# Last chunk of a two-layer AdaLN kernel: each tile's first expert leaves PSUM through ScalarE, the other seven stay on VectorE

## The chip, the cores and the metric

The kernel runs on one core of one Trainium2 chip. The metric is device time in microseconds, the median of five executions. One further execution was taken with the hardware profiler; its rows are what the working below is made from. Engines are named as in the profile: PE (TensorE matmul), PEld (its weight load), DVE (VectorE), ACT (ScalarE), POOL (GpSimd), SP (SyncE; SPq is its DMA queue).

## What is computed

Two layers, each of the form x + gate * attention(norm(x)), then x + gate * mixture(norm(x)), on x of 4 x 1024 x 256 floats. The change sits in the last mixture, that of layer 1:

```
def _L1_ffn_ref(hidden_states, router_w, expert_weights):
    x = hidden_states.reshape(-1, H)
    probs = softmax(x @ router_w.T)
    topk_vals, topk_idx = top_k(probs, 2)
    topk_w = topk_vals / (topk_vals.sum(-1) + 1e-06)
    expert_out = einsum('nh,eho->eno', x, expert_weights)     # 8 experts, 256 x 256 each
    combined = the two chosen experts' rows of expert_out
    out = ((combined + their probs) * topk_w).sum(over the two)
...
x = x + gb * _L1_ffn_ref(h, ...)
```

For a token the result is a sum over the two chosen experts of weight times row, plus one number per token (the two probabilities times their weights), times the gate.

## The kernel before, in words

Tokens are handled in 8 chunks, numbered 0 to 7, of 4 tiles; a tile is 128 tokens (one on each partition) of 256 features, one for each of the four batch rows b. `x_sb` holds all of x on the chip.

Layer 1's mixture goes two ways. Chunks 0 to 3 (group "ga") and 4 to 6 (group "gb") are **routed**: their normalised rows are written to DRAM (`ga_rows`, `gb_rows`), sorted by expert into blocks of 128, and each block is fetched by a gather, multiplied by one expert's weights (PE, L2276), copied out of PSUM by ACT (L2286) and stored to DRAM (`gb_y`, SP, L2289). When all blocks of a group are stored, `combine` takes every tile back: two gathers on POOL (L332) fetch each token's two rows into a buffer `yg`, ACT scales the first and adds the bias (L1504), and DVE adds the second (L1510), multiplies by the gate (L1513) and adds into `x_sb` (L1515). Then SP stores the chunk (L2464, 512 KB). There are five `yg` buffers; group gb has 12 tiles, so 24 gathers.

Chunk 7 is **dense** (function `dense`): for each of its four tiles, PE multiplies by all eight experts, two at a time, into a PSUM tile `p_e` of 2 x 256 (L2324, four groups j of four matmuls per tile; three such PSUM buffers). DVE takes the experts out one after the other into a tile `step`: expert 0 by a TENSOR_SCALAR that multiplies by the token's weight `d_w` and adds the bias `d_vb` (L2340), experts 1 to 7 by a SCALAR_TENSOR_TENSOR that multiplies by the weight and adds the running sum (L2349). Then `done` multiplies by the gate and adds into `x_sb` (L2369, L2370) and SP stores the tile (L2373, 128 KB). There are two `step` buffers, so tile b needs tile b - 2 to be done.

The order on every engine is fixed when the kernel is built. A planner (`Plan`) holds pieces of work, each with an engine, a cost in us, the pieces it comes after, the buffers it holds and a rank; it plays them through and emits the instructions in the order in which the pieces would begin. Each engine then works its own list in that order, and semaphores hold an instruction whose input is not ready. The costs in the planner only decide the order. Dense tiles and the combines of chunks 4 to 6 are interleaved on DVE in this way.

Of the kernel before, what the change touches and what calls it, by code (L numbers as in the profile page):

```python
# [11 lines left out]
AF = mybir.ActivationFunctionType  # L12
ALU = mybir.AluOpType
# [6 lines left out]
P = 128  # L20
B, S, D = 4, 1024, 256
# [117 lines left out]
def adaln_d2_kernel(  # L139
# [20 lines left out]
    nc = tc.nc  # L160
# [10 lines left out]
    def psum(pool, shape, name):  # L171
        tag = {id(ps_1): "p1", id(ps_2): "p2", id(ps_m): "pm"}[id(pool)]
        t = pool.tile([P, 512], F32, tag=tag, name=name)
        n = 1
        for s in shape[1:]:
            n *= s
        v = t[: shape[0], :n]
        if len(shape) == 3:
            v = v.rearrange("p (a b) -> p a b", b=shape[2])
        return v  # L180
# [61 lines left out]
    rank = const.tile([P, E], F32, name="rank")  # L242
# [636 lines left out]
    plan = Plan(p1=3, p2=2, pm=3, xn1=5, h1T=2, xn2=6, h2T=2, t1=1)  # L879
    PE, ACT, DVE, POOL = "PE", "ACT", "DVE", "POOL"  # L880
# [408 lines left out]
    ps = plan.slot("p1")  # L1289
# [27 lines left out]
    for half in range(2):  # L1317
        ps = plan.slot("p1")
# [11 lines left out]
        m = plan(PE, 0.3, turn, after=routes, holds=[ps], rank=rank_)  # L1330
# [6 lines left out]
    for piece in range(3):  # L1337
        ps = plan.slot("p2")
        m = loaded
        for k in range(KD):  # L1340
# [12 lines left out]
            m = plan(PE, 0.87, mm, after=[m, of_batch["routed"]], holds=[ps], rank=20.0)  # L1353
# [5 lines left out]
    ps = plan.slot("p1")  # L1359
    d = of_batch["turned"]  # L1360
    m = plan(PE, 0.2, lambda: g0.total_staged(ps_1), after=[d], holds=[ps], rank=-1.0)
    ps2 = plan.slot("p1")

    def bases():
# [8 lines left out]
        after=[m2],  # L1373
        holds=[ps2],
        rank=-0.9,
    )
    ps = plan.slot("p1")
    m = plan(PE, 0.4, lambda: g0.across(ps_1), after=[d], holds=[ps], rank=-1.0)
# [3 lines left out]
    for j in range(AHEAD):  # L1382
        ps = plan.slot("p1")
# [12 lines left out]
        m = plan(PE, 0.25, look, after=[r], holds=[ps], rank=first)  # L1396
        plan(DVE, 0.6, find, after=[m], holds=[ps], rank=first)
        kept_busy(0.7 if j < AHEAD - 1 else 2.0, [m], 30.0 + j)
    with tc.manual_schedule(engines=ORDERED):
# [36 lines left out]
        step=2,  # L1436
# [6 lines left out]
    made = {}  # L1443
# [7 lines left out]
    def tiny(shape, tag, n=2, dt=F32):  # L1451
        return home["tiny"].tile(shape, dt, tag=tag, name=tag, bufs=n)
# [310 lines left out]
    plan = Plan(rings=RINGS, **room1)  # L1763
# [184 lines left out]
    plan = Plan(rings=RINGS, **room1)  # L1948
# [199 lines left out]
    def shares(g, c, at, vb, x, rank):  # L2148

        key = ("m", c)  # L2150

        def do():
            x = made[key, "x"]
            down = tiny([P, B, E + 1], "rdown")
            nc.vector.tensor_scalar(down, x, -1.0, 1.0, ALU.mult, ALU.add)
            nc.vector.reciprocal(down, down)
            nc.vector.scalar_tensor_tensor(x, x, 1.0, down, ALU.add, ALU.mult)
            p = tiny([P, 2, B], "rp")
            nc.vector.tensor_reduce(p[:, 0, :], x[:, :, :E], AX.X, ALU.add)
            nc.vector.reciprocal(p[:, 0, :], p[:, 0, :])  # L2160
            nc.vector.tensor_tensor(
                p[:, 1, :].unsqueeze(2), x[:, :, E : E + 1], p[:, 0, :].unsqueeze(2), ALU.mult
            )
            total = tiny([P, B], "rtotal")
            nc.vector.scalar_tensor_tensor(
                total, p[:, 0, :], 1e-6, p[:, 1, :], ALU.add, ALU.add
            )
            nc.vector.reciprocal(total, total)
            w = g.w[:, :, at : at + B]
            nc.vector.tensor_tensor(  # L2170
                w, p, total.unsqueeze(1).to_broadcast([P, 2, B]), ALU.mult
            )
            nc.vector.tensor_tensor(p, p, w, ALU.mult)
            nc.vector.tensor_tensor(vb[:, at : at + B], p[:, 0, :], p[:, 1, :], ALU.add)

        return plan(DVE, 2.2, do, after=[x[0]], holds=[x[1]], rank=rank)
# [119 lines left out]
    def dense(c, slotT, ts, d, x, rank):  # L2296

        key = ("d", c)
        g = last_pairs
        vb = tiny([P, B], "d_vb", 1)  # L2300
        x = shares(g, c, 0, vb, x, rank)

        def spread_w():
            w = made[key, "w"] = tiny([P, B, E], "d_w", 1)
            v = tiny([P, B, E], "d_v", 1)
            for i, t in ((0, w), (1, v)):
                nc.vector.tensor_tensor(
                    t,
                    g.one[:, i, :, :],
                    g.w[:, i, :].unsqueeze(2).to_broadcast([P, B, E]),  # L2310
                    ALU.mult,
                )
            nc.vector.tensor_tensor(w, w, v, ALU.add)

        x = plan(DVE, 0.6, spread_w, after=[x, d], rank=rank)
        for b in range(B):
            last, st = [], plan.slot("step")
            for j in range(E // 2):
                ps = plan.slot("p1")

                def mm(b=b, j=j):
                    p1 = made[key, b, j] = psum(ps_1, [P, 2, D], "p1_e")
                    for k in range(KD):
                        nc.tensor.matmul(  # L2324
                            p1,
                            lhsT=made["n2", c, "hT"][:, k, b, :],
                            rhs=ew[:, 2 * j : 2 * j + 2, k, :],
                            start=(k == 0),
                            stop=(k == KD - 1),
                        )  # L2330

                def out_(b=b, j=j):
                    if j == 0:
                        made[key, "sum", b] = tiny([P, D], "step")
                    w, sum_ = made[key, "w"], made[key, "sum", b]
                    for i in range(2):
                        e = 2 * j + i
                        p = made[key, b, j][:, i, :]
                        if e == 0:
                            nc.vector.tensor_scalar(  # L2340
                                sum_,
                                p,
                                w[:, b, e : e + 1],
                                vb[:, b : b + 1],
                                ALU.mult,
                                ALU.add,
                            )
                        else:
                            nc.vector.scalar_tensor_tensor(  # L2349
                                sum_, p, w[:, b, e : e + 1], sum_, ALU.mult, ALU.add  # L2350
                            )

                m = plan(
                    PE, 1.74, mm, after=ts, holds=[ps, slotT], rank=rank + 0.1 * b + 0.02 * j
                )
                last = [
                    plan(
                        DVE,
                        0.95,
                        out_,  # L2360
                        after=[m, x, *last],
                        holds=[ps, st],
                        rank=rank + 0.1 * b + 0.02 * j - 0.5,
                    )
                ]

            def done(b=b):
                sum_, xs = made[key, "sum", b], x_sb[:, c, b, :]
                nc.vector.tensor_tensor(sum_, sum_, mods1[GB][:, b, :], ALU.mult)  # L2369
                nc.vector.tensor_tensor(xs, xs, sum_, ALU.add)  # L2370

            def store(b=b):
                nc.sync.dma_start(out[b, c * P : (c + 1) * P, :], x_sb[:, c, b, :])  # L2373

            f = plan(DVE, 0.9, done, after=last, holds=[st], rank=rank + 0.1 * b)
            plan(SP, 0.1, store, after=[f], rank=rank)
# [10 lines left out]
    for c in range(NC):  # L2387
# [26 lines left out]
        if c == NC - 1:  # L2414
            d, x = routed(last_pairs, c, 0, slotT, ts, 7.46)
            dense(c, slotT, ts, d, x, 8.23)
            continue
        g, first = groups[which], 4 * which
        at = (c - first) * B
        d, x = routed(g, c, at, slotT, ts, c + 1.05)  # L2420
# [108 lines left out]
```

## Time and profile before

| | us |
|---|---|
| median of 5 executions | 1129.64 (1128.33 to 1131.09) |
| the profiled execution: device time | 1129.15 |
| the profiled execution: span, first to last instruction | 1127.4 |
| PE busy in the span | 1088.8 (97%) |
| DVE busy | 588.2 (52%) |
| ACT busy | 424.5 (38%) |
| POOL busy | 422.2 (37%) |

All times of the profile count from the start of the span. A group's row gives line, engine, operation, output and inputs, the tile's shape, the count, and the mean duration. Consecutive instructions of an engine overlap by some 0.1 us, so that the distance from start to start is a little off the duration. PE's shares are those of the whole span; the stretch that the change touches is the last 45 us, where PE ends at about 1113.5 us.

### The profile page before, as it was taken

To read this page: it belongs to the slowest core of one execution; us is meant where nothing else is said; L and a number is where in the kernel's file an instruction comes from. 1 tells how busy PE (TensorE), PEld (TensorE's weight loads), DVE (VectorE), ACT (ScalarE), POOL (GpSimd) and SP (SyncE) were. 2 spreads that over 40 slices of the span, in tenths; PEclk is the share of its full clock that TensorE was granted. 3 is DMA by queue.
4 is the path that set the end of the run, shared out by engine and by line. 5 is a ranking of instruction groups with operands and counts; after the bars stand their busy time and mean duration, and the time that the engine had idled before them with its cause. 6 is when DMAs were issued, how large, how long until landed. Compare 5 with 4: busy or idle time off the path is not lost.

```text
span 1127.4 us, 18450 instructions
## 1 busy us (share of the span) xinstructions
PE 1088.8 (97%) x6231; PEld 867.7 (77%) x6231; DVE 588.2 (52%) x2305; ACT 424.5 (38%) x1148; POOL 422.2 (37%) x483
## 2 busy tenths in 40 slices
PE   8999999999999999999999999999999999999994
PEld 5896899999999999999989565675656667656761
DVE  7777332222222222222256488968577635698567
ACT  6976233332233322333244333423224425342431
POOL 1000455555555555555554010100114422654635
PEclk9999999999999999999999999999999999999998
DMA  9424449433331514242161221100003323432544
GB/s 320 162 54 95 151 143 315 149 117 113 100 130 38 189 39 150 78 145 86 38 238 54 72 57 57 60 25 19 1 31 97 117 71 82 133 117 75 167 108 147
DMA packets 77692, 122.38 MB, mean 109 GB/s; under 512 B 27340, under 2 KB 57301, under 8 KB 72990
## 3 DMA queue, kind: packets, MB, share of 16 engines
q0 software_dynamic: 31872, 69.68, 19.6%
q1 hardware_dynamic: 44622, 49.92, 13.8%
q10 hardware_dynamic: 1104, 1.58, 0.4%
q8 instruction: 52, 0.85, 0.3%
q14 instruction: 42, 0.34, 0.1%
HBM read 205.25 MB, written 30.22 MB: 209 GB/s over the span
## 4 chain that ended last, share of the span: by engine, by line
PE 83%; DVE 8%; DMA 4%; ACT 2%; issue 2%; SPq 1%; POOL 0%; DVEq 0%; ACTq 0%
PE p_h L1658 20%; PE p_y L1681 20%; PE p_u L1967 19%; PE p_f L2015 10%; PE p_e L2276 4%; PE pm_x L2259 1%; PE pm_x L1638 1%; DMA w<-in_W,g_wrow 1%; PE pm_l L2107 1%; PE pm_t L1620 1%; PE pm_counts L737 1%; PE pm_l L1233 1%; PE pm_o L1193 1%; DVE yg L1510 1%; DVE step L2349 1%
## 5 line engine op out<-in xcount | busy, mean ns | idle before, releaser
L1670 ACT ACTIVATE hid<-p_h,w 128x128 f32<-128x128 f32 x544 | 154.9, 368 | 326.4 <-issue 249.0
L1658 PEld LDWEIGHTS p_h<-xT,w 128*128 128x128 f32 x2176 | 253.1, 192 | 5.8 <-DVE xT L1643 1.9
L1658 PE MATMUL p_h<-xT,w 128*128 128x128 f32 x2176 | 254.4, 275 | 1.9 <-DVE xT L1643 1.3
L1681 PE MATMUL p_y<-w,hid 128*128 128x256 f32 x1088 | 248.9, 382 | 0.0
L1967 PE MATMUL p_u<-hT,a 128*128 128x512 f32 x512 | 230.8, 595 | 1.1 <-ACTq L1930 0.8
L1681 PEld LDWEIGHTS p_y<-w,hid 128*128 128x128 f32 x1088 | 201.6, 190 | 24.6
L1967 PEld LDWEIGHTS p_u<-hT,a 128*128 128x128 f32 x512 | 94.3, 190 | 97.7 <-issue 88.3
L332 POOL DMA_INDIRECT w<-in_W,g_wrow x134 | 135.0, 1008 | 74.7 <-ACT hid L1670 46.9
L784 POOL DMA_INDIRECT y<-y,g_dest x68 | 69.5, 1022 | 146.9 <-DVE g_reached L724 111.8
L1643 DVE COPY xT<-pm_x 128x256 f32<-128x256 f32 x68 | 28.8, 424 | 179.5 <-PE pm_x L1638 179.5
L1692 DVE TENSOR_TENSOR y<-p_y,w 128x256 f32<-128x256 f32 x68 | 28.8, 424 | 175.8 <-PE p_y L1681 175.8
L2015 PE MATMUL p_f<-a,hf 128*128 128x256 f32 x512 | 116.1, 380 | 0.0
L332 POOL DMA_INDIRECT xg<-h_rows,g_row x68 | 66.7, 980 | 122.9 <-DVE g_hits L750 102.5
L2015 PEld LDWEIGHTS p_f<-a,hf 128*128 128x128 f32 x512 | 96.2, 190 | 17.7 <-issue 5.7
L2063 POOL TENSOR_TENSOR x_sb<-x_sb,step 128x256 f32<-128x256 f32 x32 | 24.4, 764 | 173.5 <-DVE step L2056 120.5
L332 POOL DMA_INDIRECT xg<-ga_rows,ga_row x39 | 37.2, 954 | 91.4 <-DVE ga_row L759 35.0
L2276 PE MATMUL p_e<-ew,xT 128*128 x280 | 70.5, 384 | 0.3 <-ACT y L2286 0.3
L1979 ACT ACTIVATE hf<-p_u,decay 128x512 f32<-128x512 f32 x56 | 38.1, 684 | 78.2 <-PE p_u L1967 74.5
L2276 PEld LDWEIGHTS p_e<-ew,xT 128*128 128x128 f32 x280 | 49.3, 190 | 9.5 <-issue 3.5
L1578 DVE TENSOR_TENSOR h<-h,mod 128x256 f32<-128x256 f32 x128 | 51.4, 426 | 8.2 <-ACT h L1568 5.9
L1983 DVE SCALAR_TENSOR_TENSOR hf<-p_u,decay,hf 128x512 f32<-128x512 f32 x56 | 41.9, 748 | 22.7 <-PE p_u L1967 15.4
L2286 ACT COPY y<-p_e 128x256 f32<-128x256 f32 x70 | 25.9, 371 | 59.6 <-PE p_e L2276 27.9
(362 smaller groups left out, 1281.6 us busy)
## 6 DMA issues: line engine op xcount, KB each, us to landing
yg<-y SPq DMA_DIRECT2D x32, 256.0 KB, 2.5
ga_y<-y SPq DMA_DIRECT2D x39, 128.0 KB, 1.7
x_sb<-in_x SPq DMA_DIRECT2D x8, 512.0 KB, 7.5
h_rows<-xn SPq DMA_DIRECT2D x8, 512.0 KB, 3.5
gb_y<-y SPq DMA_DIRECT2D x31, 128.0 KB, 1.8
out_x<-x_sb SPq DMA_DIRECT2D x7, 512.0 KB, 3.6
a<-in_fw SPq DMA_DIRECT2D x6, 512.0 KB, 9.5
mod<-mod_rows SPq DMA_DIRECT2D x6, 512.0 KB
```

The costliest lines, as they stand in the source:

```text
L332: return nc.gpsimd.indirect_dma_start(out=dst, out_offset=None, in_=table, in_offset=bass.IndirectOffsetOnAxis(ap=index, axis=0), bounds_c ...
L784: nc.gpsimd.indirect_dma_start(out=table, out_offset=bass.IndirectOffsetOnAxis(ap=dest, axis=0), in_=y, in_offset=None, bounds_check=2 * s ...
L1578: nc.vector.tensor_tensor(h, h, mods1[(sc, sh)[i]][:, b, :], (ALU.mult, ALU.add)[i])
L1643: nc.vector.tensor_copy(xT, pt)
L1658: nc.tensor.matmul(p1[:, i, :], lhsT=w1[:, k * H + m * P : k * H + (m + 1) * P], rhs=xT[:, k, :], start=(k == 0), stop=(k == KD - 1),)
L1670: nc.scalar.activation(hid[:, m, :], p1[:, i, :], AF.Relu, bias=w1buf[j % 2][:, KD * H + m : KD * H + m + 1],)
L1681: nc.tensor.matmul(p2, lhsT=hid[:, m, :], rhs=w2[:, m * D : (m + 1) * D], start=(m == 0), stop=(m == KH - 1),)
L1967: nc.tensor.matmul(pu, lhsT=a[:, k, m * P : (m + 1) * P], rhs=made["n1", c, "hT"][:, k, :, :], start=(k == 0), stop=(k == KD - 1),)
L1979: nc.scalar.activation(made[key, m], made[key, m, 0], AF.Silu, scale=decays[c])
L1983: nc.vector.scalar_tensor_tensor(h, made[key, m, 1], decays[c], h, ALU.mult, ALU.mult)
L2015: nc.tensor.matmul(made[key, "p2", b], lhsT=made[key, m][:, b * P : (b + 1) * P], rhs=a1[:, m, :], start=(m == 0), stop=(m == KH - 1),)
L2276: nc.tensor.matmul(made[key, "p2"], lhsT=made[key, "xT"][:, k, :], rhs=ew_flat[:, bass.ds(made[key, "at"] + k * D, D)], start=(k == 0), st ...
```

## The change

In `dense`, expert 0 of each of the four tiles is no longer taken out of PSUM by DVE. A new piece `begin` on ACT does it: one ACTIVATE (Identity) with the token's weight as scale and the bias as bias, both one number per partition, from PSUM into `step`. It is planned at 0.45 us, after the first matmul group and the shares, and holds the same PSUM and `step` buffers. DVE's piece for j = 0 comes after it and holds one instruction (expert 1) in place of two; its planned cost goes from 0.95 to 0.48.

```diff
+                def begin(b=b):
+                    sum_ = made[key, "sum", b] = tiny([P, D], "step")
+                    nc.scalar.activation(
+                        sum_,
+                        made[key, b, 0][:, 0, :],
+                        AF.Identity,
+                        bias=vb[:, b : b + 1],
+                        scale=made[key, "w"][:, b, 0:1],
+                    )
+
                 def out_(b=b, j=j):
-                    if j == 0:
-                        made[key, "sum", b] = tiny([P, D], "step")
                     w, sum_ = made[key, "w"], made[key, "sum", b]
                     for i in range(2):
                         e = 2 * j + i
                         p = made[key, b, j][:, i, :]
-                        if e == 0:
-                            nc.vector.tensor_scalar(
-                                sum_, p, w[:, b, e : e + 1], vb[:, b : b + 1],
-                                ALU.mult, ALU.add,
-                            )
-                        else:
+                        if e:
                             nc.vector.scalar_tensor_tensor(
                                 sum_, p, w[:, b, e : e + 1], sum_, ALU.mult, ALU.add
                             )
...
+                if j == 0:
+                    last = [
+                        plan(ACT, 0.45, begin, after=[m, x], holds=[ps, st],
+                             rank=rank + 0.1 * b - 0.5)
+                    ]
                 last = [
                     plan(
                         DVE,
-                        0.95,
+                        0.95 if j else 0.48,
                         out_,
                         after=[m, x, *last],
                         holds=[ps, st],
```

In the order that the planner then emits, everything up to the dense chunk stands as before. On ACT the four new instructions (L2334 in the changed file) stand ahead of the last L2286 copy, behind the first combine's L1504, between those of the third and the fourth, and behind that of the seventh. On DVE the four L2340 are gone, and near the end two pieces move up: `done` of the third dense tile goes ahead of the tenth combine, and `done` of the fourth ahead of the eleventh, so that the list ends with two combines. POOL, PE and SP keep their order.

More of the change, by code (lines that the diff above doesn't have):

```diff
@@ L2338, in out_ @@
                         p = made[key, b, j][:, i, :]
-                        if e == 0:
[L2340 to L2346, printed above, removed]
-                            )
-                        else:
+                        if e:
                             nc.vector.scalar_tensor_tensor(
@@ L2355, in dense @@
                 )
+                if j == 0:
+                    last = [
+                        plan(
+                            ACT,
+                            0.45,
+                            begin,
+                            after=[m, x],
+                            holds=[ps, st],
+                            rank=rank + 0.1 * b - 0.5,
+                        )
+                    ]
                 last = [
```

## The prediction

> **What bounds the kernel now.** I read the page first (PE is busy 97% of the span, so only the end can belong to another engine), then the windows of the last 45 us, then the chain of waits and the timelines of DVE, POOL, ACT and SP there. The windows (stretch and length; busy us of PE, PEld, DVE, ACT, POOL; PE clock; DMA share; GB/s):
>
> ```profile
> 1085.00:1091.00 6.00, 6.00 (x17) 2.84 (x16) 3.13 (x7) 0.37 (x1) 1.96 (x3) 1.00 0.15 47
> 1091.00:1110.00 19.00, 18.56 (x44) 7.93 (x42) 17.89 (x42) 4.80 (x8) 14.67 (x15) 1.00 0.46 138
> 1110.00:1123.00 13.00, 1.95 (x4) 0.68 (x4) 11.97 (x28) 2.40 (x4) 6.80 (x7) 0.78 0.48 151
> 1123.00:1127.40 4.40, 0.00 (x0) 0.00 (x0) 0.00 (x0) 0.00 (x0) 0.00 (x0) 0.50 0.36 121
> ```
>
> Up to 1091 PE sets the pace; from 1091 to 1123 DVE is full; then only the last store runs. The DVE timeline (start, duration) shows where the four removed instructions sit and what surrounds them:
>
> ```profile
> 1084.89 0.54 DVE L2340 TENSOR_SCALAR step<-p_e,d_w,d_vb 128x256 f32<-128x256 f32 x1
> 1085.47 0.48 DVE L2349 SCALAR_TENSOR_TENSOR step<-p_e,d_w,step 128x256 f32<-128x256 f32 x1
> 1087.29 1.00 DVE L2349 SCALAR_TENSOR_TENSOR step<-p_e,d_w,step 128x256 f32<-128x256 f32 x2 [1.33 <-PE p_e L2324]
> ...
> 1092.56 0.53 DVE L2340 TENSOR_SCALAR step<-p_e,d_w,d_vb 128x256 f32<-128x256 f32 x1
> 1093.13 0.48 DVE L2349 SCALAR_TENSOR_TENSOR step<-p_e,d_w,step 128x256 f32<-128x256 f32 x1
> ...
> 1110.35 0.54 DVE L2340 TENSOR_SCALAR step<-p_e,d_w,d_vb 128x256 f32<-128x256 f32 x1
> ...
> 1121.35 0.48 DVE L1510 SCALAR_TENSOR_TENSOR yg<-yg,gb_w 128x256 f32<-128x256 f32 x1
> ...
> 1122.32 0.43 DVE L1515 TENSOR_TENSOR x_sb<-x_sb,yg 128x256 f32<-128x256 f32 x1
> ```
>
> In the first tile DVE then waits for PE, so time saved there is handed to that wait. From 1092.56 on DVE waits for nobody. But a second row of work runs beside it to almost the same end. POOL's gathers (in brackets: idle time before, and who ended it) and ACT's last step:
>
> ```profile
> 1088.43 0.95 POOL L332 DMA_INDIRECT yg<-gb_y,gb_slot  x1 [13.80 <-DMA gb_y<-y]
> ...
> 1116.56 1.00 POOL L332 DMA_INDIRECT yg<-gb_y,gb_slot  x1 [0.30 <-DVE yg L1510]
> 1117.86 1.01 POOL L332 DMA_INDIRECT yg<-gb_y,gb_slot  x1 [0.30 <-issue]
> ```
>
> ```profile
> 1119.58 0.60 ACT L1504 ACTIVATE yg<-yg,gb_vb,gb_w 128x256 f32<-128x256 f32 x1 [2.11 <-DMA yg<-gb_y,gb_slot]
> ```
>
> The answer for the tile yg adds how long a gather takes from issue to landing:
>
> ```profile
> DMA to landing us min/median/max: 2.7/2.8/3.3
> ```
>
> POOL never stops: 24 gathers, always 0.30 us apart whoever is named for it, 29.43 us from first start to last, 1.28 each. They start when the last block is stored and depend on no DVE work that this change makes later. The last gather starts at 1117.86 and lands between 1120.56 and 1121.16, by the median at 1120.66. DVE takes its rows at 1121.35. So DVE ends the kernel, with only 0.2 to 0.8 us between it and the gathers. That is the number that the forecast turns on.
>
> **The change, step by step.** *Removed on DVE.* Four L2340, 0.57 us from start to next start (1092.56 to 1093.13). All on the path they would be worth 2.3 us. Tile by tile:
> - Tile 1: ACT begins when DVE did, 1084.89 or some hundredths later (both need `d_w`). Its duration is in no row of before. Nearest are L1504, 0.60 us (same size, both operands from memory, SBUF source), and L1019, 0.77 us (PSUM source, both operands, twice the elements); from below the L2286 copy, 0.37 us (PSUM source, no operands). I take 0.57, the 0.60 row less a little, since only the source differs. Expert 1 then starts at about 1085.5, as before, and DVE waits for PE at 1087.29 anyway. Gain 0.
> - Tile 2: PE's groups release DVE at 1087.29, 1089.00 and 1090.72 in the timeline, 1.72 apart, so the next is ready at 1092.44. ACT runs 1092.44 to 1093.01 (free since its L1504 at 1091.14), DVE continues at about 1093.03 instead of 1093.13. Gain 0.1; between 0.3 (0.37 row) and -0.1 (0.77 row).
> - Tiles 3 and 4: PE is ahead (their first groups are ready four and eight groups of 1.72 later, near 1099.3 and 1106.2; DVE wants them at 1100.4 and 1110.35). ACT fits in: for tile 3 at 1099.3; for tile 4 after the `step` buffer of tile 2 is freed, its `done` ending at 1109.1 less the 0.67 gained by then, so 1108.5 to 1109.1, while DVE is busy with the seventh combine until 1109.7. Gain 0.57 each.
>
> DVE's sum is 0 + 0.1 + 0.57 + 0.57 = 1.24 us: it would be ready for the last combine at 1121.35 - 1.24 = 1120.1.
>
> *Added on ACT.* Four instructions on an engine busy 2.40 of the last 13 us. What queues behind them: the last L2286 copy behind the first, L1504 steps behind the others. The copy matters, since its store starts the gathers, and a late start would move the whole gather row one for one. It ran at 1085.61, when PE had finished its block. ACT starts the next instruction of this kind 0.50 us after the last (two L1568 in a row took 1.10), so it is free at 1085.4; even at the 0.77 row it is free at 1085.6. Cost 0, covered by that PE wait by 0.2 us. Tile 3's step delays the fourth L1504 from 1098.87 to about 1099.9, ending 1100.5; DVE wants it at 1100.7. Cost 0, covered by 0.2.
>
> *PE* waits 2.0 us for a PSUM buffer before its last group (1111.55); that buffer comes free 1.24 us sooner, the group ends near 1112.3, and DVE wants it at 1113.65. Nothing gained, nothing lost.
>
> *What is late next.* With the new order DVE's tail reads: ninth combine 1114.57, `done` of tile 3 at 1115.88, tenth combine 1116.68, `done` of tile 4 at 1117.99, eleventh combine 1118.79, free 1120.10 (1.31 per combine, 0.80 per `done`, the distances of before). The last combine then waits for the last gather; before, `done` of tile 4 stood there and hid that wait. The gather lands at 1120.66 by the median. SP's stores move too: tile 4's 128 KB go out at 1118.8 instead of 1121.5, so they now meet the last gather on the DMA engines; the store of the chunk before, 512 KB, goes from 1115.0 to 1113.9 and meets the gathers of the eleventh combine, which have over 0.6 us to spare by the median. The gather issued at 1116.56 flew right behind that 512 KB store and its ACT step began at 1119.58, 3.02 us later. I take 3.02 for the last one: 1117.86 + 3.02 = 1120.88, against 1121.35. **Gain 0.47 us**, between 0.79 (2.7) and 0.19 (3.3). What follows, three instructions and the last 512 KB store from 1122.77 to 1127.4, is unchanged.
>
> Span 1127.4 - 0.47 = 1126.9; with the 1.75 us around it, 1128.7 for that execution, which lay 0.49 under the median. On the median: 1129.64 - 0.47, about **1129.2**.
>
> [...] The 3.3 us maximum above is the trace's word on such meetings; without any meeting the sum would be 0.69, with a bad one 0.19.
>
> **Rivals.** (1) *The gather row also gets shorter, faster by more.* Gathers last 0.944 to 1.187 us; at the shortest throughout, 23 x 1.25 = 28.75 instead of 29.43, so the last starts 0.68 sooner, and the end comes up to 0.47 + 0.68, about 1.15 us sooner, near DVE's own 1.24: 1128.5. For it: less DVE work beside POOL. Against: the removed instructions read PSUM, and no row shows that they slowed a gather. (2) *The last gather lands late, slower than before.* Place: the last combine, behind tile 4's store and the gather. Price: its start less 1121.35. It decides from 3.49 us after issue. The worst in the answer is 3.3; with the excess over the median doubled (two stores met, tile 3's and tile 4's) it is 3.8, and the end 0.3 us later: 1129.9. Against: no row of that answer reaches 3.49. (3) *DVE's saving counts in full, 2.3 us*, 1127.3: excluded for tile 1 by its PE wait, and it would need the gathers another 1.2 us sooner than in rival 1.
>
> **How the numbers follow.** Forecast case (end set by the last gather, 0.2 to 0.8 us gained) 0.65; rival 1, 0.15; rival 2, 0.18; rival 3, 0.02. All but rival 3 are smaller than 0.2% (2.26 us), about what a measurement of this kernel can tell from no change; the five times of before spread over 2.8 us, so a median of five is good to about 1 us either way. The range takes rival 1 and 1 us below (1127.5) and rival 2 and 1 us above (1130.9). Beyond 0.2% only rival 3 or an unlucky pair of medians: faster 0.07, slower 0.04, within 0.89.
>
> **What would show it.** In the changed profile: no TENSOR_SCALAR on `step`; four ACT rows of about 0.57 us; DVE still waiting for PE in tile 1; PE's wait of 2.0 us shrunk to about 0.8; and, the main sign, an idle time of 0.5 to 1.1 us on DVE before the last L1510, ended by the gather's DMA, and POOL still at 1.28 per gather from 1088.4. If DVE shows no such idle time and the end is 1.2 us sooner, the gather bound is wrong; if the first gather starts after 1088.6, the ACT copy was delayed; if the last gather's rows come after 1121.35, rival 2 holds.

## The result, and the profile after

| | us |
|---|---|
| median before (46 executions) | 1129.99 |
| median after (25 executions) | 1129.55 |
| ratio after/before, 95% interval | 0.9995 [0.9989, 1.0002] |
| profiled execution after: span | 1127.9 |

The medians differ by 0.44 us where 0.47 was forecast. The interval, from 1.2 us faster to 0.2 us slower, does not tell that from no change, so it is luck that the two numbers lie so close. The finer evidence is in the profile, one execution of each kernel.

Its span is 0.5 us longer than that of before, and this must be read first: the token weights (DVE, L2313) start at 1085.39 instead of 1084.59. The order of work up to there is the same in both kernels, so those 0.80 us are the difference of two executions, not the change (the kernel before with one gather more, a run below with the same work up to there, has them at 1085.29). The comparison needs an event that both share: I count from T0, the start of the first gather of `yg`, 1088.43 before and 1089.22 after (3.84 and 3.83 us behind the token weights). The first and the last gather of the changed kernel, on POOL (start, duration, what; in brackets the idle time before):

```profile
1089.22 0.95 POOL L332 DMA_INDIRECT yg<-gb_y,gb_slot  x1 [13.79 <-DMA gb_y<-y]
...
1118.68 1.01 POOL L332 DMA_INDIRECT yg<-gb_y,gb_slot  x1 [0.30 <-issue]
```

The windows of the end of the changed kernel (stretch and length; busy us of PE, PEld, DVE, ACT, POOL; PE clock; DMA share; GB/s):

```profile
1091.00:1110.00 19.00, 19.00 (x46) 8.24 (x44) 17.08 (x40) 5.82 (x11) 14.43 (x16) 1.00 0.44 137
1110.00:1123.00 13.00, 2.34 (x5) 0.68 (x4) 11.43 (x28) 2.85 (x5) 7.56 (x8) 0.80 0.54 161
```

DVE is no longer full. Where its free time lies stands in its timeline, in the brackets:

```profile
1086.28 0.48 DVE L2348 SCALAR_TENSOR_TENSOR step<-p_e,d_w,step 128x256 f32<-128x256 f32 x1 [0.69 <-ACT step L2334]
1088.08 1.00 DVE L2348 SCALAR_TENSOR_TENSOR step<-p_e,d_w,step 128x256 f32<-128x256 f32 x2 [1.32 <-PE p_e L2324]
...
1093.83 0.48 DVE L2348 SCALAR_TENSOR_TENSOR step<-p_e,d_w,step 128x256 f32<-128x256 f32 x1 [0.40 <-ACT step L2334]
...
1120.55 0.42 DVE L1515 TENSOR_TENSOR x_sb<-x_sb,yg 128x256 f32<-128x256 f32 x1
1121.78 0.48 DVE L1510 SCALAR_TENSOR_TENSOR yg<-yg,gb_w 128x256 f32<-128x256 f32 x1 [0.81 <-DMA yg<-gb_y,gb_slot]
```

In tiles 1 and 2 DVE waits for ScalarE in place of working (0.69 and 0.40 us), and in tile 1 still for PE (1.32). Before the last combine it now waits 0.81 us for the last gather. The chain that ended last (start, length, what) names that gather:

```profile
1118.37 0.30 issue
1118.68 3.01 DMA yg<-gb_y,gb_slot
1121.69 0.03 issue
1121.72 0.02 DVEq L1510
1121.74 0.04 issue
1121.78 0.49 DVE yg L1510
```

ACT's four new instructions and the copy behind the first:

```profile
1085.68 0.56 ACT L2334 ACTIVATE step<-p_e,d_vb,d_w 128x256 f32<-128x256 f32 x1 [1.48 <-DVE d_w L2313]
1086.41 0.37 ACT L2286 COPY y<-p_e 128x256 f32<-128x256 f32 x1 [0.16 <-PE p_e L2276]
...
1093.23 0.57 ACT L2334 ACTIVATE step<-p_e,d_vb,d_w 128x256 f32<-128x256 f32 x1 [0.62 <-PE p_e L2324]
...
1100.10 0.57 ACT L2334 ACTIVATE step<-p_e,d_vb,d_w 128x256 f32<-128x256 f32 x1 [2.52 <-PE p_e L2324]
...
1109.40 0.56 ACT L2334 ACTIVATE step<-p_e,d_vb,d_w 128x256 f32<-128x256 f32 x1 [1.38 <-DVE x_sb L2380]
```

The copy whose store starts the gathers runs 1.02 us behind the token weights, exactly as before (1085.61 - 1084.59), and still waits for PE.

The start of the L1510 of some combines, counted from T0 and taken from the DVE timelines of all profiles without a standstill (more on that below; with one gather more, T0 is the start of the added one):

| us from T0 | combine 1 | 4 | 8 | 12 | last gather issued |
|---|---|---|---|---|---|
| before | 5.10 | 12.94 | 25.11 | 32.92 | 29.43 |
| after | 5.01 | 12.28 | 23.92 | 32.56 | 29.46 |
| after, four gathers fewer | 5.01 | 12.27 | 23.86 | 31.61 | |
| after, `done` moved back | 5.00 | 12.27 | 23.88 | 32.35 | 29.42 |
| after, one gather more | 5.99 | 13.25 | 25.11 | 33.80 | 30.65 |
| before, one gather more | 5.35 | 13.44 | 26.00 | 33.90 | 30.74 |

The second row against the first: 0.09 us gained at combine 1 (dense tile 2 lies ahead of it), 0.66 at combine 4 (tile 3), 1.19 at combine 8 (tile 4), and 0.36 left at combine 12. Each row of the table is one execution. The issue of the last gather, less 1.25 us where there is one more, lies between 29.40 and 29.49 us wherever it is given, so 0.36 us is clear of that scatter.

### The profile page after: what moved, and what is told of

Read it like the earlier page. It is cut to its first block, busy times and chain, and to the rows that moved or that the text cites. A ratio compares the mean times of both kernels' runs of the same rounds, so it can differ in the third digit from the quotient of the medians.

```text
span 1127.9 us, 18447 instructions
## 1 busy us (share of the span) xinstructions
PE 1090.0 (97%) x6231; PEld 868.7 (77%) x6231; DVE 586.5 (52%) x2301; ACT 426.9 (38%) x1152; POOL 423.3 (38%) x483
## 4 chain that ended last, share of the span: by engine, by line
PE 84%; DVE 8%; DMA 3%; ACT 2%; issue 2%; POOL 0%; SPq 0%; DVEq 0%; ACTq 0%
PE p_h L1658 20%; PE p_y L1681 20%; PE p_u L1967 19%; PE p_f L2015 10%; PE p_e L2276 4%; PE pm_x L2259 1%; DMA w<-in_W,g_wrow 1%; PE pm_x L1638 1%; PE pm_l L2107 1%; PE pm_t L1620 1%; PE pm_gram L1100 1%; PE pm_counts L737 1%; PE pm_l L1233 1%; PE pm_o L1193 1%; PE p_e L2324 1%
## 5 line engine op out<-in xcount | busy, mean ns | idle before, releaser
L1983 DVE SCALAR_TENSOR_TENSOR hf<-p_u,decay,hf 128x512 f32<-128x512 f32 x56 | 41.9, 748 | 22.6 <-PE p_u L1967 15.4
L2286 ACT COPY y<-p_e 128x256 f32<-128x256 f32 x70 | 26.0, 371 | 57.4 <-PE p_e L2276 25.5
```

Of the source, the lines that this page charges most:

```text
L1983: nc.vector.scalar_tensor_tensor(h, made[key, m, 1], decays[c], h, ALU.mult, ALU.mult)
```

## The experiments

**First set: gathers taken away or added.** Two questions: is DVE's saving really 1.24 us, and does the last gather hide most of it? The cut, made to both kernels:

```diff
-                    gather(made[key, c, b][:, i, :], y, g.slot[:, i, s : s + 1])
+                    if key != "c2" or c != NC - 2 or i == 0:
+                        gather(made[key, c, b][:, i, :], y, g.slot[:, i, s : s + 1])
...
+                i = 0 if key == "c2" and c == NC - 2 else 1
...
-                    t[:, 0, :], t[:, 1, :], g.w[:, 1, s : s + 1], t[:, 0, :], ALU.mult, ALU.add
+                    t[:, 0, :], t[:, i, :], g.w[:, 1, s : s + 1], t[:, 0, :], ALU.mult, ALU.add
```

> The kernel before, without the second gather of the last four combined tiles (their first row is used twice, so the output of that chunk is not the reference's); the order on every engine is kept, POOL issues 20 gathers in place of 24. Times from T0, the start of the first gather of yg. Theory (in the kernel before DVE sets the end, with the gathers 0.2 to 0.8 us behind it): the last L1510 stays at T0 + 32.9 us, as before (1121.35 - 1088.43 = 32.92), within 0.2. Rival (the gathers already set the end before): it comes earlier by as much as 0.5 us or more.

> The changed kernel with the same four gathers left out (that chunk's output is not the reference's). Theory (DVE's saving is 0 + 0.1 + 0.57 + 0.57 = 1.24 us, and in the changed kernel all but 0.36 us of it is eaten by the last gather): no idle time on DVE before the last L1510, which stands at T0 + 31.7 us, 1.24 earlier than in the run of the kernel before with the same cut, and the device time is 1.2 us (0.11%) less than that one's. Rival A (the saving itself is smaller, the new waits on ACT eat it): T0 + 32.3 to 32.6, as in the full changed kernel. Rival B (all four instructions count, 2.3 us): T0 + 30.6.

And the addition, made to both:

```diff
+                    if key == "c2" and (c, b, i) == (4, 0, 0):
+                        spare = late.tile([P, 1, D], F32, name="spare")
+                        gather(spare[:, 0, :], y, g.slot[:, 0, s + 1 : s + 2])
                     gather(made[key, c, b][:, i, :], y, g.slot[:, i, s : s + 1])
```

> The kernel before with one more gather (into a tile that nobody reads) ahead of the 24. T0 is the start of the first of the 25. Theory (gathers 0.2 to 0.8 us behind DVE): the row ends 1.25 us later, the last gather begins at T0 + 30.7 and lands 2.8 to 3.1 later, so the last L1510 moves from T0 + 32.9 to T0 + 33.5 to 33.8, by 0.6 to 0.9, with a short idle time on DVE before it. Rival (the gathers are far from the end): it stays at T0 + 32.9.

> The changed kernel with the same extra gather. Theory (the last gather sets the end): the last L1510 moves by the whole 1.25 us, from T0 + 32.56 to T0 + 33.8, and DVE's idle time before it grows from 0.8 to about 2.0 us; so the two kernels with one more gather end within 0.3 us of each other. Rival (DVE or ACT sets the end of the changed kernel and the wait seen is an accident): a shift of 0.5 us or less.

These four ran where the kernel before took 1151.66 us, 22 us more than in the runs above, and their profiles show why they answer nothing. In the DVE and POOL timelines of the kernel before with four gathers fewer:

```profile
1128.19 1.00 DVE L2351 SCALAR_TENSOR_TENSOR step<-p_e,d_w,step 128x256 f32<-128x256 f32 x2 [6.66 <-remote]
```

```profile
1130.78 0.95 POOL L332 DMA_INDIRECT yg<-gb_y,gb_slot  x1 [4.67 <-DVE x_sb L1517]
```

In the middle of the gather row DVE stands for 6.66 us, released by nothing that the profile shows ("remote"), and PE is idle there for 6.4 us; on DVE the other three show 4.7 to 8.2 us of the same. The gathers meanwhile run ahead until all `yg` buffers are full, and then it is POOL that waits for DVE; so not "all engines" stand still, as an expectation below has it. The bound under test is gone. The two kernels with four gathers fewer came out alike, 0.9975 [0.9962, 0.9989] and 0.9980 [0.9965, 0.9995] of the kernel before (the expected 1.2 us between them would be 0.11%, less than these intervals resolve); the two with one gather more gave 1152.3 and 1151.88 in one run each. Inconclusive.

**Second set: the same again, and the order of the tail.** It ran where the kernel before took 1130.77 us; no standstill shows in any of its profiles. The device times, one run each, are 1132.31 and 1130.83 us with one gather more (changed kernel, kernel before), 1128.71 with four fewer and 1130.37 with the order moved back; single runs of one kernel spread over more than that, so the rows decide.

> The changed kernel without the second gather of the last four combined tiles (that chunk's output is not the reference's), once more. Theory: without the gather bound DVE shows its 1.24 us: no idle time before the last L1510, which stands 31.7 us after the first gather's start (the kernel before: 32.9; the changed kernel: 32.56). Rival A (the waits on ACT eat the saving): 32.3 to 32.6. Rival B (all four instructions count): 30.6.

The last L1510 (L1512 in that file) of the changed kernel with four gathers fewer, from the DVE timeline:

```profile
1120.54 0.42 DVE L1517 TENSOR_TENSOR x_sb<-x_sb,yg 128x256 f32<-128x256 f32 x1
1120.88 0.48 DVE L1512 SCALAR_TENSOR_TENSOR yg<-yg,gb_w 128x256 f32<-128x256 f32 x1
```

No idle time, and 1120.88 - 1089.27 = 31.61 us from T0, 1.31 before the 32.92 of the kernel before. The saving is there in full, and both rivals fall. Of the 0.95 us that the changed kernel lacks (32.56 - 31.61), 0.81 are its wait for the last gather and about 0.1 the overlap of two instructions that the wait prevents; 0.06 was there at combine 8 already.

> The changed kernel with one more gather ahead of the 24, once more: in the first run all engines stood still for 6.8 us in the middle of the gather row, which the profiles of the two kernels do not show, so that POOL had caught up before the end. Without such a standstill, theory (the last gather sets the end): the last L1510 moves from 32.56 to 33.8 us after the first gather's start, and DVE's idle time before it grows from 0.8 to 2.0 us. Rival (DVE or ACT sets the end): a shift of 0.5 us or less.

> The kernel before with one more gather, once more for the same reason. Theory (gathers 0.2 to 0.8 us behind DVE): the last L1510 moves from 32.9 to 33.5 to 33.8 us after the first gather's start, half the shift of the changed kernel, and the two kernels end within 0.3 us of each other. Rival (the gathers are far from the end): 32.9.

The changed kernel moved by the whole 1.24 us, to 33.80; the kernel before by 0.98, to 33.90, 0.1 us beyond the 33.5 to 33.8 expected; they end within 0.1 us of each other. So with the gathers 1.25 us later the change is worth nothing. One part of both expectations failed: where DVE waits. In the changed kernel with one gather more the wait before the last combine is 0.85 us, not 2.0:

```profile
1096.27 0.48 DVE L2351 SCALAR_TENSOR_TENSOR step<-p_e,d_w,step 128x256 f32<-128x256 f32 x1 [1.37 <-ACT step L2337]
...
1124.48 0.48 DVE L1513 SCALAR_TENSOR_TENSOR yg<-yg,gb_w 128x256 f32<-128x256 f32 x1 [0.85 <-DMA yg<-gb_y,gb_slot]
```

Most of the rest was lost at tile 2, where DVE waits 1.37 us for ScalarE in place of 0.40, and some 0.2 us between the fourth and the eighth combine (the table). ScalarE's new instruction is queued behind the first combine's scaling, and that waits for the first gather: a late gather now reaches DVE's dense work through ScalarE's queue. In the changed kernel itself that instruction waits 0.62 us for PE after the scaling, so the cover is 0.62 us. In the kernel before with one gather more DVE waits 0.16 us at the first and 0.29 at the seventh combine, and no wait is marked before the last. By the table 0.89 of its 0.98 us are lost by the eighth combine, step by step, part of them in gaps too short to be marked; at the expected place, the last combine, it is about 0.1 us.

The order of the tail, with the last tile's `done` after the eleventh combine again:

```diff
-            f = plan(DVE, 0.9, done, after=last, holds=[st], rank=rank + 0.1 * b)
+            wait = [combined[-2]] if b == B - 1 else []
+            f = plan(DVE, 0.9, done, after=[*last, *wait], holds=[st], rank=rank + 0.1 * b)
...
+    combined = []
...
+                combined[:] = done
```

> The changed kernel with the last tile's done (and its 128 KB store) put back between the eleventh and the twelfth combine, as in the kernel before; nothing else differs. Theory (that store, pulled forward, meets the last gather): the last gather lands 2.8 to 2.9 us after its issue in place of 3.0, the last L1510 stands 32.3 to 32.4 us after the first gather's start, 0.2 sooner than in the changed kernel, and DVE's idle time before it is near 0. Rival (the meeting costs nothing): it stays at 32.55.

The chain that ended last of this kernel:

```profile
1119.60 2.84 DMA yg<-gb_y,gb_slot
1122.44 0.03 issue
1122.47 0.02 DVEq L1510
1122.49 0.04 issue
1122.53 0.49 DVE yg L1510
```

The last gather takes 2.84 us where it took 3.01, and the last L1510 stands at 32.35 instead of 32.56. The only store that changed its place is the last tile's, the second of the two in this row of SP's queue, in the changed kernel and then here:

```profile
1117.58 2.44 SPq L2383 DMA_DIRECT2D out_x<-x_sb  x2
```

```profile
1118.50 4.07 SPq L2383 DMA_DIRECT2D out_x<-x_sb  x2
```

It is issued by 1120.02, in the flight of the last gather (1118.68 to 1121.69), and here by 1122.57, when the gather has landed (1122.44). In the changed kernel with one gather more, where the store stays forward, the last gather took 3.06 us. So the meeting seems to cost about 0.2 us, by one execution with the store moved back. The same shows at tile 2's store of 128 KB: the ninth combine's first gather, issued within 0.3 us of it, takes 2.9 to 3.0 us to land in four profiles, where gathers with no store near take mostly 2.7 to 2.8. But one of these took 3.2 (issued at 1090.47 in the changed kernel), so the size is not certain. The idle time was 0.32 us, not near 0, and 0.23 us at the eleventh combine: there DVE waits for ScalarE, held by a gather that took 3.7 us beside the 512 KB store. In the changed kernel that gather went out at 1114.74 and the store at:

```profile
1114.56 0.38 SPq L2474 DMA_DIRECT2D out_x<-x_sb  x1
```

**Third set: a smaller last store.** After the last combine only a store is left, so its size is on the path: the last routed chunk is stored tile by tile, in the kernel before and in the changed kernel with `done` moved back.

```diff
+                if q == NC - 2:
+                    for b in range(B):
+
+                        def tile_store(q=q, b=b):
+                            nc.sync.dma_start(
+                                out[b, q * P : (q + 1) * P, :], x_sb[:, q, b, :]
+                            )
+
+                        plan(SP, 0.1, tile_store, after=[done[b]], rank=8.2 + 0.2 * (q - first))
+                    continue
+
                 def store(q=q):
...
```

> The changed kernel with the last tile's done put back between the last two combines (as in the run before) and the last routed chunk stored tile by tile, four 128 KB stores in place of one of 512 KB. Theory (what follows the last combine is the last store alone, and a 128 KB store lands in 1.9 us where a 512 KB one takes 3.6): the last L1510 still 32.35 us after the first gather's start, and the time from there to the end of the span falls from 6.1 us by 1.3 to 1.7; on the device time, with the 0.5 us of the change and the 0.2 of the order, about 2.0 us under the kernel before (ratio 0.998). Rival (the three early tile stores meet the last gathers and give the time back): the last L1510 at 33.0 or later, ratio 0.9995 or more.

> The kernel before with the last routed chunk stored tile by tile. Theory: DVE sets the end here, so the last L1510 stays at 32.9 us after the first gather's start, and only the last store gets shorter, by 1.3 to 1.7 us: ratio 0.9987. The difference to the run of the changed kernel with the same stores, 0.5 to 0.7 us, is what the change is worth. Rival (store size does not matter): ratio 1.000.

> As the first of these, with the chunk before it also stored tile by tile, so that no 512 KB store meets the gathers of the eleventh combine. Theory: in the changed kernel that store held one gather up to 3.7 us; without it the eleventh combine waits for nothing, but the end hangs on the last gather, so the time is that of the first run within 0.3 us. Rival (the 512 KB store also delays the last gather): another 0.3 us or more gained.

> The changed kernel with ScalarE taking the first expert of dense tiles 3 and 4 only (tiles 1 and 2 as before), and without the second gather of the last four combined tiles, so that the gathers do not set the end (that chunk's output is not the reference's). Theory (tile 1 is worth 0, tile 2 0.1): the last L1510 stands 31.6 to 31.75 us after the first gather's start, the same as with all four tiles on ScalarE (31.61). Rival (every tile is worth its 0.57): 32.7.

These ran where the kernel before took 1148.14 us, again with standstills in the gather row (DVE waits of 4.0 to 6.1 us marked "remote", one or two in each). The T0 marks of the last combine are therefore useless (41.9, 43.2 and 42.2 us), and what is expected of these marks is not tested. The tail behind the last combine is. For the changed kernel with tile stores, DVE and SPq:

```profile
1140.25 0.42 DVE L1515 TENSOR_TENSOR x_sb<-x_sb,yg 128x256 f32<-128x256 f32 x1
```

```profile
1140.70 0.33 SPq L2480 DMA_DIRECT2D out_x<-x_sb  x1
```

Its span ends at 1143.6, 2.9 us after DVE's last instruction; before it was 4.65 (1122.75 to 1127.4), and 4.7 in the run of this set that keeps the 512 KB store. That is 1.7 us, the upper end of the 1.3 to 1.7 expected. Device times as shares of the kernel before: 0.9964 [0.9949, 0.9979] for the changed kernel with the moved `done` and tile stores; 0.9973 [0.9957, 0.9989] for the kernel before with tile stores; 0.9967 [0.9950, 0.9985] for the first of these with two chunks stored by tiles. All three intervals lie below 1, and the first two ratios below the expected 0.998 and 0.9987, which lie at the edge of the one interval and inside the other; the changed kernel as it is did not run in this set. The store is worth more than the change: 1.7 us against 0.36 in the profiles. The 0.8 us between the first two (1145.21 and 1146.04) lie in the expected direction, but their intervals overlap. The run with two chunks is not told from the run with one.

The run with ScalarE in tiles 3 and 4 only (tiles 1 and 2 have DVE's TENSOR_SCALAR again) cannot be read at its end either (a standstill of 5.4 us), but it can be read part by part. Combine 1, behind tile 2, stands at 5.10 us from T0, as in the kernel before, against 5.01 with ScalarE: tile 2 is worth 0.09. From the third to the fourth combine, with tile 3 between them, it takes 1.70 us against 2.28 before; from the seventh to the eighth, with tile 4, 3.92 against 4.50. Each of these two is worth 0.58. Its expected mark for the last combine (31.6 to 31.75 us) is not tested.

## Why the prediction was right, step by step

- *Tile 1 worth 0, tile 2 worth 0.1, tiles 3 and 4 worth 0.57 each.* Measured 0.09 at the first combine, 0.57 more at the fourth, 0.53 more at the eighth in the changed kernel; in sum 1.31 at the end where the gathers do not bind, against 1.24 forecast. In tile 1 DVE waits 1.32 us for PE as before.
- *ScalarE's instruction, 0.57 us.* It takes 0.566, the mean of the four L2334, whose scale and bias are both read from memory; the copy L2286, which has neither, takes 0.37. With 0.37, by the prediction's estimate, tile 2 would have gained 0.3, and it gained 0.09.
- *The copy and its store not delayed.* The first gather starts 3.83 us behind the token weights, 3.84 before. By the span's own clock two signs of the prediction read the other way: the first gather starts after 1088.6 (1089.22), and the last gather's rows come after 1121.35 (1121.69). Both were set against one execution's clock; less the 0.80 us by which this execution was late before the dense chunk, neither holds.
- *PE's wait.* It shrank from 1.99 to 0.70 us (0.8 forecast), and nothing came of it.
- *The last gather sets the end.* DVE is free at 32.56 - 0.81, about 31.75 us from T0, and then idle for 0.81 us (0.5 to 1.1 forecast); the end is the gather's. The 3.02 us of the forecast ran from the issue of another gather to the start of the instruction that reads its rows; the same distance is 3.10 us for the last gather here (1118.68 to 1121.78), of which 3.01 to its landing. The last gather was also issued 0.03 us later from T0. So the gain in the trace is 32.92 - 32.56 = 0.36 us, against 0.47. That one gather's time fitted another so well is in part luck: without tile 4's store beside it the last gather took 2.84 us, and the eleventh combine's first gather took 3.7, more than the 3.3 that the prediction had as the worst and more than the 3.49 at which its rival 2 begins.
- *Tile 4's store meets the last gather.* Moving it back took 0.17 us off, from 3.01 to 2.84 us between issue and landing, in one execution. That agrees with a store that slows a gather beside it, and so does the 3.7 us gather beside the 512 KB store; in what way the one holds up the other no run here shows.
- *The rivals.* The gather row did not get shorter (29.46 us, 29.43 before), so rival 1 falls: with four instructions fewer on DVE, POOL's row stayed as it was. The last gather stayed under 3.49 us, so rival 2 did not occur, and with one gather more in front both kernels end alike, not the changed one later. Nor did the saving count in full (rival 3): 1.31 us at most, in the run with four gathers fewer.
- *What was missed.* The prediction worked out what is queued behind ScalarE's new instructions. Of what they are queued behind it noted only that the first combine's scaling was done in time for tile 2, not that this scaling waits for a gather and how late that may come. Here it cost nothing, by a cover of 0.62 us; with one gather more it cost 0.97. And the eleventh combine's cover was thinner than the "over 0.6 us" of the prediction: its gather took 3.7 us and left ScalarE done at 1119.06, with DVE coming at 1119.58.

## What to carry to other kernels

Before taking work off a full engine, look at the second row of work that ends beside it: here the gain was what lay between DVE and the last gather (0.36 us), not the four instructions removed. A piece of other work that stands just before a wait hides it (before the last combine DVE waited 0.81 us without tile 4's `done` there and 0.32 with it), so look at what a scheduler moves when a cost changes. And what followed DVE's last instruction was on the path in full, 4.65 us with the 512 KB store and 2.9 with tile stores: a final store cut to a quarter of its size was worth more (1.7 us) than DVE's whole saving from the four instructions (1.31 us where the gathers do not bind).

## What the runs showed of the hardware

Two of the three sets ran where the same kernel before takes 18 to 22 us longer, and where DVE stands still for 4 to 8 us at a time inside the rows of back-to-back gathers (3.97 to 8.18 us, "remote"), released by nothing in the profile. In the first set PE is idle for 3.8 to 8.5 us there, while POOL goes on until its buffers are full and then waits for DVE, 4.67 us in the first run. It shows in one such row of the earlier routed group too: 6.45 us on DVE at 982.77 in the first run. What stops them is open; the three sets ran on three different chips, so the chip or the session may matter, and no run here separates them. It was only seen that a bound worth half a microsecond cannot be measured across such a standstill, because the row that was late has time to catch up.

A gather was slower here close to a 512 KB store. In the profiles without a standstill the five gathers whose landing is known and that were issued between 0.5 us before and 0.7 us after a 512 KB store took 3.6 to 4.0 us; four issued 1.1 to 1.5 us after one took 2.9 to 3.3, and one issued 0.9 us ahead of it took 2.7, like most others. Why it depends on the distance in this way was not tested.
